# Row sums of softmax numerators: from full columns on 128 partitions to folded strips of 64 rows by 32 columns

## The chip, the cores and the metric

The kernel runs on one core of a Trainium2 chip. The metric is the time of one execution on the device in microseconds (us), of which three runs were made. Five engines work side by side, each on its own queue in order: PE (TensorE, with its weight loads as PEld), DVE (VectorE), ACT (ScalarE), POOL (GpSimd) and SP (SyncE, here only for issuing DMAs).

## What is computed

Four graph layers on 32 samples of 512 nodes with 256 features, all in fp32, each behind a layernorm and a relu and added to its input:

```python
h = max(layernorm(x), 0); x = x + attention(h, adj)            # layer 0: 4 heads of 64
h = max(layernorm(x), 0); x = x + two_gats_with_mlps(h, adj)   # layer 1
h = max(layernorm(x), 0); x = x + gat(h, adj, 4 heads of 64)   # layer 2, elu at the end
h = max(layernorm(x), 0); x = x + gat(h, prior=adj, 8 heads of 32) @ W_out.T   # layer 3
```

In each of them softmax numerators p (node j by node i, for each head) are multiplied with values, and the result is divided by the sums of p over j. The change is about those sums in layers 0, 2 and 3.

## The kernel before

A sample is worked on feature-major: tiles of 128 partitions by 512 nodes. For one head, p is four tiles p[j], with j on the partitions (four blocks of 128) and the 512 nodes i along the free dimension. The product with the values contracts over the partitions, four matmuls into one PSUM bank (`av`). The row sums contract in the same way with a matrix of ones: first the four p[j] are added elementwise to one tile, `total`, and then one matmul with 32 columns of ones gives the 512 sums on 32 partitions. Four heads take four column strips of the array, so four such matmuls fill one bank `sm` (a unit of four; in the profile eight passes, since an fp32 product takes two).

The names and lines to follow:
- `layer0` (L694): for m in 0, 1, two heads each: scores `sc` in two row strips of 64, exp on ACT, the mask and the additions to `total` on DVE, the products `av` in two column strips of 64. Then one `sm` unit for all four heads and `normalise`.
- `normalise` (L669): copies `sm` and `av` out of PSUM, sends the sums through DRAM to 128 partitions (`s1`, `few`), inverts them, sends them back (`s2`) and out to all partitions (`rc`), and multiplies.
- `separable` (L858), for layers 2 and 3: for each group g of four heads (one group in layer 2, two in layer 3) and each j, ACT makes exp tiles from the broadcast `R`, DVE takes the maximum with the second branch and masks. For g = 0 the additions to `total` are DVE's; for g = 1 they are accumulating DMAs that POOL issues, into p[0] (`p<-p` in the profile). The last sample of layer 2 and the last two of layer 3 take the sums directly from the p[j] with ones on TensorE (`direct`).
- `norm_t` (L609): layernorm; its power of -0.5 (`rs`) is a POOL instruction.

The order of the work is not the order of this code. Every operation is recorded as a step (`Plan`, L71) and `Plan.order` (L157) chooses, with costs from `cost` (L319), the step that can start first, ties by a due time; a sample's due time is its number times `PERIOD`, less the work behind the step and less a number from the table `URGENT`. Samples and layers are released at `STARTS`, `PACE` and `LAYERS`. At most `AHEAD` + 1 samples are in flight. A step that opens a new tile has to get a buffer: 62 common SBUF blocks of 128 by 512, eight PSUM banks, 4 tiles x of a sample's residual; some are held back for older samples (`KEEP`, `OWN`). All instructions are then issued in that order (`issue`, L267), so that nearly all carry line L283.

Of the kernel before, what the change touches and what calls it, by code (L numbers as in the profile page):

```python
# [43 lines left out]

PERIOD = 179.0
STARTS, PACE = (0.0, 0.0, 38.0, 159.0), 85.0
LAYERS = (0.0, 4.0, 2.0, 98.0)

URGENT = {
    "pt:0": 192, "mm:0": 49, "total:0": 70, "av:0": 68, "mm:1": 25, "total:1": -78, "rs1:1": 42, "av:1": -7,  # L50
    "p2:1": 104, "p3:2": -95, "total:2": -542, "ue:2": -396, "mv:3": -121, "mm:3": -158, "p3:3": -723,
    "av:3": -527, "total:3": -695,
}
BLOCKS, KEEP = 62, 2
KEEP_BANKS = 0
# [15 lines left out]
class Plan:  # L71
# [8 lines left out]
    ENGINES = dict(tensor="PE", vector="DVE", scalar="ACT", gpsimd="POOL", sync="SP")  # L80
    HOP, AHEAD = 0.05, 3

    OWN = dict(block=8, bank=2)

    SWITCH = dict(full=0.094, columns=0.12, rows=0.2)
# [71 lines left out]
    def order(self):  # L157
# [35 lines left out]
        def slots(step):  # L193

            when, taken = 0.0, {}
            for name in step.touches:
                if name in live:
                    continue
                tag = self.tile_tag[name]
                keep = self.tags[tag][1]  # L200
                reserve = 0
                for s in range(oldest, step.sample):
                    if to_come[s].get(tag, 0):
                        reserve += max(0, min(keep, to_come[s][tag] + held.get((s, tag), 0)) - held.get((s, tag), 0))
                n = taken.get(tag, 0)
                own = self.OWN.get(tag, 0)
                if own:
                    passed = bisect_left(pending[step.sample, tag], place[name]) - n
                    reserve += max(0, min(own, passed))
                if len(free[tag]) - n <= reserve:  # L210
                    return None
                when = max(when, sorted(free[tag])[n])
                taken[tag] = n + 1
            return when
# [104 lines left out]
def cost(engine, op, args, kw, out):  # L319
# [22 lines left out]
    if engine == "POOL":  # L342
        if op == "dma_start":
            return 1.1, (5.2 if n == N else 8.0)
        return (1.0 if n < 16 else 0.683), 0.1
# [7 lines left out]
def gnn_stack_kernel(ctx: ExitStack, tc: tile.TileContext, a: dict, out: bass.AP):  # L353
# [66 lines left out]
    def new_x():  # L420
        return first.tile([P, NT, D], F32, name="x", bufs=4)

# [160 lines left out]
    def pipelined(stack):  # L583
# [15 lines left out]
        def small(name, *free):  # L599
            return q.tile(big, [P, *free], name, 4)  # L600

        def half(b, t):

            return b[t // 2][:, t % 2 * D : (t % 2 + 1) * D]
# [64 lines left out]
        def normalise(avs, sm):  # L669


            raws, sums = blocks("raw", len(avs)), block("sums")
            q.scalar.copy(sums, sm)
            for raw, av in zip(raws, avs):
                q.scalar.copy(raw, av)
            s1, s2 = q.tile(dram, [4, N], "s1", 8), q.tile(dram, [4, N], "s2", 8)
            q.sync.dma_start(s1, sums[0:P:32, :])
            few = small("few", 2, 4 * NT)
            c = 4 * N // P
            q.sync.dma_start(few[:, 0, :], T(s1, "h (p c) -> (h p) c", c=c))  # L680
            q.vector.reciprocal(few[:, 1, :], few[:, 0, :])
            q.sync.dma_start(T(s2, "h (p c) -> (h p) c", c=c), few[:, 1, :])
            dst = blocks("oT", len(avs))
            per = 4 // len(avs)
            for i, raw in enumerate(raws):
                rc = block("rc")
                for h in range(per):
                    f = P // per
                    q.sync.dma_start(rc[h * f : (h + 1) * f, :], s2[i * per + h : i * per + h + 1, :].to_broadcast([f, N]))
                q.vector.tensor_tensor(dst[i], raw, rc, op=ALU.mult)  # L690
            return dst


        def layer0(xt):  # L694
            hT = norm_t(xt)
# [11 lines left out]
            rows = [slice(0, 64), slice(64, P)]  # L707
            avs, totals = [], []
            for m in range(KD):
                av = bank("av")  # L710
                avs.append(av)
                tot = blocks("total", 2)
                totals += tot
                p = {}
                for jj in range(0, NT, 2):
                    for j in (jj, jj + 1):
# [4 lines left out]
                        for s in range(2):  # L721
# [3 lines left out]
                            if j:  # L725
                                q.vector.tensor_tensor(tot[s], p[0, s] if j == 1 else tot[s], b, op=ALU.add)
                    with q.unit("columns", 1.72):
                        for j in (jj, jj + 1):
                            for s, r in enumerate(rows):
# [3 lines left out]
                                )  # L733
            sm = bank("sm")
            with q.unit("columns", 0.86):
                for n, b in enumerate(totals):
                    q.tensor.matmul(sm[n * 32 : n * 32 + 32, :], ones[:, :32], b, start=True, stop=True)
            oT = normalise(avs, sm)
            for t in range(0, NT, 2):
# [118 lines left out]
        def separable(xt, w, nh, mask, bars):  # L858
# [16 lines left out]
            q.sync.dma_start(T(rd[:nh, :], "h (t p) -> t h p", p=P), rT[: NT * nh, :])  # L875
            per = P // f
            for g in range(nh // 4):
                R = blocks("R", 4)
# [3 lines left out]
                direct = q.left <= (1 if nh == H2 else 2)  # L882
                total = blocks("total", 4) if g == 0 and not direct else None
                sm = bank("sm") if direct else None
                for j in range(NT):
                    p = blocks("p3", 4)
                    for s in range(4):
# [4 lines left out]
                        )  # L892
                        if j and total:
                            q.vector.tensor_tensor(total[s], first[s] if j == 1 else total[s], p[s], op=ALU.add)
                        elif j and not direct:
                            q.gpsimd.dma_start(out=first[s], in_=p[s], accum_op=ALU.add)
                    if not j:
                        first = p
                    st = dict(start=(j == 0), stop=(j == NT - 1))
                    with q.unit("columns", (0.86 if per == 4 else 1.72) + (0.86 if direct else 0)):  # L900
# [3 lines left out]
                        if direct:  # L904
                            for s in range(4):
                                q.tensor.matmul(sm[s * F3 : (s + 1) * F3, :], ones[:, :F3], p[s], **st)
                if not direct:
                    sm = bank("sm")
                    with q.unit("columns", 0.86):
                        for s, b in enumerate(total or first):  # L910
                            q.tensor.matmul(sm[s * F3 : (s + 1) * F3, :], ones[:, :F3], b, start=True, stop=True)
                bars(g, avs, sm)

        def layer2(xt):
            y = blocks("y3", 3)

            def bars(g, avs, sm):
                for b, ps in zip(y, avs + [sm]):
                    q.scalar.copy(b, ps)

            separable(xt, w2, H2, mask1T, bars)
# [17 lines left out]
        def layer3(xt):  # L939
            oT = []  # L940

            def bars(g, avs, sm):
                if q.left > 1:
                    oT.extend(normalise(avs, sm))
                    return
# [79 lines left out]
        for i in range(B):  # L1025
            q.begin()
            q.sample, q.left = i, B - i
            xt = q.adopt(new_x() if i else x0, "x", 4)
            if i:
# [434 lines left out]
```

## Time and profile before

| | |
|---|---|
| three runs | 3959.78, 3960.19, 3964.37 us; median 3960.19 |
| span of the profiled execution | 3962.9 us |
| mean granted TensorE clock | 0.992 |
| PE, DVE, ACT, POOL busy | 98%, 84%, 71%, 14% of the span |
| row sums after additions (`sm<-total`, `sm<-p`) | 1144 passes, 8 in a unit |
| POOL's accumulating DMAs `p<-p` | 360 |
| DMA traffic | 292.57 MB |

The profile is of one execution, whose span from first to last instruction stands in the second row, beside the times of the three runs. In its lines, an instruction is named by what it writes and reads (`sm<-total,ones`), with rows*columns of the array and the shapes; "x8" is a count; busy time is in us, the mean of one in ns. In the table of stretches each line has the stretch, its length, the busy time of PE, PEld, DVE, ACT and POOL with the number of instructions, the granted clock, the DMA share and GB/s. The timeline has start, length and what ran, with equal neighbours merged; two neighbours can overlap by the end of the pipeline, so that starts are compared with starts.

### The profile page before, as it was taken

How to read it: one execution, taken by the hardware profiler on the slowest of the kernel's cores; microseconds unless marked ns; L12 is line 12 of the kernel's file. 1: busy time of each engine (PE TensorE's matmuls, PEld its weight loads, DVE VectorE, ACT ScalarE, POOL GpSimd, SP SyncE). 2: the span in 40 equal slices, each digit the busy share in tenths (PEclk: the TensorE clock that was granted, in tenths of full speed). 3: DMA queues.
4: the chain of work that ended last, by engine and by line, in shares of the span. 5: the costliest groups of instructions: out<-in, count | busy, mean ns of one | idle time of the engine just before them, and what ended most of it. 6: DMA issues, size and time to landing. Idle time of an engine off the chain costs nothing.

```text
span 3962.9 us, 52558 instructions
## 1 busy us (share of the span) xinstructions
PE 3890.9 (98%) x17144; PEld 2149.1 (54%) x17144; DVE 3344.2 (84%) x7049; ACT 2805.9 (71%) x5968; POOL 566.4 (14%) x530
## 2 busy tenths in 40 slices
PE   8999999999999999999999999999999999999997
PEld 4655555555555555555555555555555555555552
DVE  6499898888888888988888988888888889888886
ACT  4577677766677766767766777666777667777665
POOL 0001111101111111111101111011111011111010
PEclk8999999999999999999999999999999999999998
DMA  3013333313233223333223333132332233332231
GB/s 101 21 37 81 72 82 84 92 44 92 57 89 92 71 65 76 76 84 84 67 63 78 76 88 88 49 89 59 86 92 73 63 76 76 84 83 69 71 77 50
DMA packets 217616, 292.57 MB, mean 74 GB/s; under 512 B 49915, under 2 KB 103422, under 8 KB 217334
## 3 DMA queue, kind: packets, MB, share of 16 engines
q0 software_dynamic: 68864, 111.18, 16.1%
q1 hardware_dynamic: 148196, 177.69, 14.3%
q8 instruction: 138, 2.26, 0.2%
q14 instruction: 144, 1.18, 0.1%
q10 hardware_dynamic: 274, 0.26, 0.0%
HBM read 158.79 MB, written 19.10 MB: 45 GB/s over the span
## 4 chain that ended last, share of the span: by engine, by line
PE 69%; DVE 17%; DMA 5%; ACT 4%; issue 2%; POOL 2%; SPq 1%; DVEq 0%; ACTq 0%; POOLq 0%
PE mm L283 33%; PE av L283 22%; PE sc L283 5%; PE pt L283 5%; DVE total L283 5%; DVE p L283 5%; DMA R<-rd 4%; PE sm L283 3%; ACT p L283 2%; POOL rs L283 2%; DVE o L283 1%; DVE ue L283 1%; DVE stats L283 1%; DVE x L283 1%; DVE y L283 1%
## 5 line engine op out<-in xcount | busy, mean ns | idle before, releaser
L283 ACT ACTIVATE p<-R,e 128x512 f32<-128x512 f32 x1536 | 993.4, 727 | 53.2 <-DMA R<-rd 52.3
L283 PE MATMUL av<-p,v 128*128 128x512 f32 (+1 forms) x2560 | 930.8, 596 | 4.5 <-DVE p L283 4.4
L283 DVE SCALAR_TENSOR_TENSOR p<-p,e,mask3T 128x512 f32<-128x512 f32 x1024 | 720.5, 749 | 8.1 <-ACT p L283 8.1
L283 POOL TENSOR_TENSOR rs<-ve,mhalf 128x4 f32<-128x4 f32 x128 | 202.5, 1582 | 2755.9 <-DVE ve L283 2634.4
L283 PEld LDWEIGHTS av<-p,v 128*128 128x128 f32 (+1 forms) x2560 | 348.2, 169 | 446.5 <-issue 357.2
L283 DVE TENSOR_TENSOR total<-total,p 128x512 f32<-128x512 f32 x872 | 572.6, 687 | 1.4
L283 PE MATMUL av<-p,vs 128*32 128x512 f32 (+1 forms) x3072 | 504.5, 598 | 5.6 <-DVE p L283 5.4
L283 PE MATMUL mm<-W_fc,o 128*128 128x256 f32 (+1 forms) x2048 | 468.4, 380 | 2.8 <-ACT o L283 2.8
L283 PEld LDWEIGHTS mm<-W_fc,o 128*128 128x128 f32 x2048 | 382.5, 190 | 85.3 <-issue 29.4
L283 POOL DMA_DIRECT2D p<-p x360 | 323.9, 1047 | 564.2 <-PE av L283 191.2
L283 DVE SCALAR_TENSOR_TENSOR p<-p,e,mask1T 128x512 f32<-128x512 f32 x512 | 350.7, 748 | 41.0 <-ACT p L283 40.4
L283 ACT ACTIVATE h<-x,ms,rs 128x256 f32<-128x256 f32 x512 | 280.1, 628 | 122.9 <-DVE ms L283 121.0
L283 DVE TENSOR_TENSOR p<-p,mask0T 128x512 f32<-128x512 f32 x512 | 328.5, 690 | 17.4 <-ACT p L283 17.2
L283 PEld LDWEIGHTS av<-p,vs 128*32 128x32 f32 (+1 forms) x3072 | 138.4, 118 | 342.2 <-issue 238.6
L283 DVE TENSOR_TENSOR total<-p,p 128x512 f32<-128x512 f32 x436 | 288.7, 687 | 0.0
L283 ACT ACTIVATE p<-sc 128x512 f32<-128x512 f32 x512 | 254.3, 679 | 7.8 <-PE sc L283 7.8
L283 PE MATMUL mm<-w,hT 128*128 128x272 f32 (+1 forms) x1024 | 254.4, 393 | 0.9 <-ACT hT L283 0.8
L283 PE MATMUL mm<-hT,mlp_w 128*128 128x512 f32 x512 | 237.6, 596 | 0.0
L283 PE MATMUL mm<-o,mlp_w 128*128 128x512 f32 x512 | 234.7, 596 | 1.3
L283 PE MATMUL sc<-qT,kT 64*128 64x512 f32 x1024 | 230.1, 599 | 0.0
L283 PEld LDWEIGHTS mm<-w,hT 128*128 128x128 f32 x1024 | 190.6, 191 | 61.0 <-issue 15.3
L283 ACT COPY rc<-pt 128x512 f32<-128x512 f32 x64 | 37.4, 585 | 246.8 <-PE pt L283 246.7
(183 smaller groups left out, 5457.5 us busy)
## 6 DMA issues: line engine op xcount, KB each, us to landing
R<-rd SPq DMA_DIRECT2D x384, 256.0 KB
p<-p POOLq DMA_DIRECT2D x360, 256.0 KB, 5.3
x<-in_x_dram SPq DMA_DIRECT2D x32, 512.0 KB
x<-boa POOLq DMA_DIRECT2D x32, 512.0 KB, 5.5
rc<-s SPq DMA_DIRECT2D x128, 128.0 KB
out_dram<-x SPq DMA_DIRECT2D x32, 512.0 KB
rc<-s SPq DMA_DIRECT2D x248, 64.0 KB
s<-sums SPq DMA_DIRECT2D x94, 8.0 KB
```

The lines of the kernel that those rows point to most:

```text
L283: getattr(getattr(self.nc, attribute), op)(*args, **kw)
```

## The change

Ahead of the row sums, the total is folded onto half of its partitions. In layers 0 and 2 the totals of two heads stand in one tile `pair` (128 partitions, two halves i of 256 nodes, two heads, 256). `fold` issues two accumulating DMAs from POOL: for i = 0 the upper 64 partitions are added to the lower 64, for i = 1 the lower to the upper. `folded` then takes eight matmuls of 64 rows, 32 columns and 256 nodes, two row strips by four column strips, into two banks. In layer 3, group g's totals are folded onto half g, and the row sums of both groups are taken together, in one unit of eight matmuls of 512 nodes; `normalise8` does the two groups in one.

Beside that, the planner's numbers change: 48 common blocks, 6 pairs (two blocks in size each) and 5 tiles x in place of 62 blocks and 4 tiles x; one more sample in flight; four blocks and two banks kept spare while an older sample still needs some; other release times and a longer table `URGENT`; and another cost of a POOL DMA. So all instructions get another order.

```diff
-PERIOD = 179.0
-STARTS, PACE = (0.0, 0.0, 38.0, 159.0), 85.0
-LAYERS = (0.0, 4.0, 2.0, 98.0)
+PERIOD = 193.0
+STARTS, PACE = (0.0, 0.0, 46.0, 123.0), 94.0
+LAYERS = (0.0, 8.0, 88.0, 61.0)
...
-BLOCKS, KEEP = 62, 2
+BLOCKS, KEEP = 48, 2
+PAIRS = 6
+LOW = slice(0, 64), slice(64, 128)
...
-    HOP, AHEAD = 0.05, 3
+    HOP, AHEAD = 0.05, 4
...
+    SPARE = dict(block=4, bank=2)
...
+                if any(to_come[s].get(tag, 0) for s in range(oldest, step.sample)):
+                    reserve += self.SPARE.get(tag, 0)
...
-            return 1.1, (5.2 if n == N else 8.0)
+            return 1.1, 3.9 + n * out.ap[0][1] * 4 / 190e3
...
-        return first.tile([P, NT, D], F32, name="x", bufs=4)
+        return first.tile([P, NT, D], F32, name="x", bufs=5)
...
+        def pair(name):
+            b = q.tile(big, [P, 2, 2, N // 2], name, PAIRS, keep=2, tag="pair")
+            return b, [b[:, :, s, :] for s in range(2)]
+        def wide(b):
+            return T(b, "p (i c) -> p i c", i=2)
+        def fold(b):
+            for i in range(2):
+                q.gpsimd.dma_start(out=b[LOW[i], i], in_=b[LOW[1 - i], i], accum_op=ALU.add)
+        def folded(pairs):
+            sm = [bank("sm"), bank("sm")]
+            with q.unit("columns", 0.44):
+                for n in range(4):
+                    for i, r in enumerate(LOW):
+                        q.tensor.matmul(
+                            sm[i][n * F3 : (n + 1) * F3, : N // 2], ones[r, :F3], pairs[n // 2][r, i, n % 2, :],
+                            start=True, stop=True,
+                        )
+            return sm
...
-            q.scalar.copy(sums, sm)
+            if isinstance(sm, list):
+                for i in range(2):
+                    q.scalar.copy(sums[:, i * D : (i + 1) * D], sm[i][:, :D])
...
+        def normalise8(raws, sms):
+            s1, s2 = q.tile(dram, [2, 4, N], "s1x", 3), q.tile(dram, [2, 4, N], "s2x", 3)
+            for g, sm in enumerate(sms):
+                sums = block("sums")
+                q.scalar.copy(sums, sm)
+                q.sync.dma_start(s1[g], sums[0:P:32, :])
+            few = small("fewx", 2, 8 * NT)
...
-            sm = bank("sm")
-            with q.unit("columns", 0.86):
-                for n, b in enumerate(totals):
-                    q.tensor.matmul(sm[n * 32 : n * 32 + 32, :], ones[:, :32], b, start=True, stop=True)
-            oT = normalise(avs, sm)
+                fold(both)
+            oT = normalise(avs, folded(totals))
...
-                            q.gpsimd.dma_start(out=first[s], in_=p[s], accum_op=ALU.add)
+                            q.gpsimd.dma_start(out=total[s], in_=p[s], accum_op=ALU.add)
...
+                    raw = block("raw")
+                    q.scalar.copy(raw, avs[0])
+                    for b in both:
+                        q.gpsimd.dma_start(out=b[LOW[g]], in_=b[LOW[1 - g]], accum_op=ALU.add)
+                    late.append((raw, total))
+            if late:
+                sms = [bank("sm"), bank("sm")]
+                with q.unit("columns", 0.86):
+                    for s in range(4):
+                        for g, r in enumerate(LOW):
+                            q.tensor.matmul(
+                                sms[g][s * F3 : (s + 1) * F3, :], ones[r, :F3], late[g][1][s][r, :],
+                                start=True, stop=True,
+                            )
+                bars(0, [raw for raw, _ in late], sms)
```

## The prediction

> **What bounds the kernel now.** I read the page's table of engines first, then the busy time by stretches, then TensorE's timeline in the middle of the run, then the groups of instructions.
>
> ```profile
> PE 3890.9 (98%) x17144; PEld 2149.1 (54%) x17144; DVE 3344.2 (84%) x7049; ACT 2805.9 (71%) x5968; POOL 566.4 (14%) x530
> ```
> ```profile
> 0.00:100.00 100.00, 84.56 (x333) 43.62 (x334) 59.52 (x152) 44.72 (x82) 9.62 (x16) 0.90 0.36 102
> ...
> 1000.00:1500.00 500.00, 498.24 (x2208) 273.61 (x2205) 435.36 (x905) 367.92 (x791) 79.76 (x76) 1.00 0.33 76
> ...
> 3800.00:3900.00 100.00, 86.18 (x430) 38.41 (x427) 81.98 (x187) 62.73 (x134) 3.04 (x3) 0.94 0.14 44
> 3900.00:3963.00 63.00, 41.24 (x187) 19.77 (x187) 33.67 (x47) 25.57 (x52) 0.00 (x0) 0.80 0.20 61
> ```
>
> Between 200 and 3800 us TensorE is busy 99.6% of the time at full clock, VectorE 87%, ScalarE 74%. So the middle is TensorE's; a microsecond of it removed is a microsecond gained until something else is late. Only the first 200 and the last 160 us are set by chains.
>
> ```profile
> 2000.17 0.27 PE L283 MATMUL pt<-ident,mx 128*128 128x128 f32 x1
> 2000.37 1.06 PE L283 MATMUL sm<-p,ones 128*32 128x512 f32 x8
> 2001.36 11.82 PE L283 MATMUL av<-p,vs 128*64 128x512 f32 x64
> 2013.00 2.02 PE L283 MATMUL sm<-total,ones 128*32 128x512 f32 x8
> 2014.95 1.53 PE L283 MATMUL pt<-ident,y 128*128 128x128 f32 x12
> ...
> 2027.29 7.03 PE L283 MATMUL av<-p,v 128*128 128x512 f32 x16
> 2034.16 0.59 PE L283 MATMUL mm<-woT,oT 128*128 128x256 f32 x2
> ...
> 2052.12 1.07 PE L283 MATMUL sm<-total,ones 128*32 128x512 f32 x8
> 2053.01 1.90 PE L283 MATMUL av<-p,vs 128*32 128x512 f32 x16
> ```
>
> Three prices come from these starts. Sixteen 512-column passes take 6.87 us, 0.429 each; a product is two passes, so four products side by side in four column strips have 0.853 us of streaming. The unit at 2052.12 is followed by one of the same array shape after 0.89: 0.037 us over, for the staggered starts. The unit at 2000.37 is followed by another shape after 0.99: a change of array shape costs about 0.095 us. At 2013.00 the unit takes 1.95, though it has the same work: it waits about 1 us for its totals.
>
> **Row sums: streaming removed.** The program has 32 row-sum units in layer 0, 31 in layer 2 and 60 in layer 3, 123 in all, besides 20 that the last samples take directly and that stay. Before: 123 x 0.853 = 105.0 us. After: layers 0 and 2 sum 256 columns in eight strips of 64 rows by 32 columns, 63 x 0.427 = 26.9; layer 3 has one unit of 512 columns in eight strips in place of two of four, 30 x 0.853 = 25.6. Saved: 52.5 us, if eight strips run at once. The trace shows two row strips at once (scores) and four column strips at once, not both.
>
> ```profile
> L283 PEld LDWEIGHTS sm<-p,ones x8: 106/108/109, 2000.4 to 2000.4; 128*32 128x32 f32 x8
> L283 PE MATMUL sm<-p,ones x8: 592/605/617, 2000.4 to 2000.8; 128*32 128x512 f32 x8
> ```
>
> These are that unit's weight loads and matmuls, with the first and last start: all eight loads begin within 0.1 us, and the second four matmuls by 0.43 us after the first. A new unit has sixteen of each. Against this stands a rule of the Trainium skill ("TensorE: Matmul & The Clock Gate", Part 1, "Wait — 56ns, not 53.3ns?"): matmuls never start less than about 25 ns apart, however small. By the rule eight starts would spread 0.2 us before each round of eight is on its way, and a unit would be about 0.2 us longer, 93 x 0.2 = 19 us of the saving. The row says otherwise: the 0.037 us over four strips is 9 ns a strip; with eight, 0.074. I take the row: 93 x 0.074 - 123 x 0.037 = +2.3 us.
>
> **Changes of shape: added.** Everything else on TensorE has the same matmuls; but the order is another. Laying the orders of the two programs' TensorE instructions side by side, the array changes shape 545 times before and 812 times after: the 64x32 strips are a shape of their own, and the layer-2 products, one stretch of 64 passes at 2001.36, stand one by one among full-array work. 267 x 0.095 = +25.4 us.
>
> **The sum.** Streaming of all matmuls is 3690.7 us before (2684.6 full array, 438.6 in 64-column, 347.4 in 32-column, 218.5 in 64-row strips, 1.8 the rest), changes of shape 545 x 0.095 = 51.8; the span 3962.9 leaves 220.4 for both ends, small starts and waits. After: 3638.3 + 77.1 + 2.3 + 220.4 = 3938.1, that is 24.8 less. The span is 2.7 above the median of the runs; applied to the median, 3935.4.
>
> **What the sum puts at nothing, and its cover.** POOL's work:
>
> ```profile
> L283 POOL DMA_DIRECT2D p<-p x360 | 323.9, 1047 | 564.2 <-PE av L283 191.2 <-ACT ew L283 142.0 <-DMA p<-p 96.5
> L283 POOL TENSOR_TENSOR rs<-ve,mhalf 128x4 f32<-128x4 f32 x128 | 202.5, 1582 | 2755.9 <-DVE ve L283 2634.4 <-DVE few L283 47.7 <-DVE sq L283 36.1
> p<-p POOLq DMA_DIRECT2D x360, 256.0 KB, 5.3
> ```
>
> The change adds 128 + 124 + 120 = 372 folding DMAs. At 1.047 us each that is 389 us on POOL, 14% becoming 24%. A fold waits for its total or for the accumulating DMA before it, and behind it on POOL are the `rs` powers of the layernorms, whose h and transposes wait. But in the new order the layer-3 folds stand just after their own accumulations, the others in a group before the same sample's `rs`, which needs them anyway; so no other sample's norm is held for long. A fold lands some 5 to 7 us after issue (the row's 5.3 for the same bytes; 4 KB on each of 64 partitions may take longer). In the order there are 70 us of matmul time between layer 0's last product and its row sums, 21 us in layer 2, 11 us in layer 3. In layer 3 two landings in series (accumulate, fold: 12 to 14 us) have to fit; they begin at the last `p`, ahead of the product, so I count zero; were 2 us missing each time, 30 x 2 = 60 us would go. Without any cover one fold is 6 us in each of 93 places.
>
> DMA traffic grows by 252 x 131 KB + 120 x 262 KB = 64 MB on 293 MB, and queues are busy 31% of the time. VectorE has the same additions, now on two pieces of 256; ScalarE takes four half copies for two full ones in layers 0 and 2, (4 x 0.41 - 2 x 0.586) / 2 = 0.23 us a unit, 15 us at 71% busy. The layer-3 normalisation sends fewer small DMAs through SP, two a sample less. All that is covered by TensorE's 99.6%; uncovered it is 15 us at most, and below nothing only where the row sums' own wait of 1 us (2013.00) disappears, as the row sums now stand 21 us after the last product: at most 31 x 1 = 31 us.
>
> The ends: the last samples keep the direct sums, and from the last sample's layer 2 on TensorE has 56 us of matmul time before and 60 after, in the same chain that takes 107 us (3855.5 to 3962.9). The start has the same loads and the first samples in nearly the same order, one fold more. Zero, 10 us either way.
>
> **Rivals.**
> (a) The sum, 3935. Its own range is 3922 to 3948.
> (b) The waits of the row sums go too and nothing takes their place: 3935 less most of the 31 us, 3910. For it: the distances above. Against: a wait ended leaves TensorE early at the next tight place.
> (c) New small waits eat what was won, within 8 us of before: 3958.
> (d) Slower: banks. Row sums hold two PSUM banks instead of one, five samples share eight. Counting matmul time between the last matmul of a bank's old content and the first of its new one, no reuse in the middle has under 2 us in the old order; in the new, eight per sample have, the shortest 1.5. Emptying takes 0.17 us of matmul end (592 ns recorded for 427 of streaming), 0.586 of copy, and 0.727 if one exponential stands ahead on ScalarE: 1.48. If these eight wait 0.2 us each beyond what they do now, 51 us: 3986. It decides from 24.8 / 32 = 0.78 us of new waits per sample. Against it: ScalarE is idle a quarter of the time, and a late TensorE lets it catch up.
> (e) The strips don't run eight at once, but in two rounds: the 52.5 us come back, 3988.
>
> **How the numbers follow.** (a) 0.48, (b) 0.20, (c) 0.10, (d) 0.17, (e) 0.05. I take 0.2%, 8 us, as what a measurement of this kernel can tell from no change. Faster: (a), (b) and part of (c), 0.70; same 0.10; slower 0.20. The range reaches from 3902 (somewhat under (b), if the ends gain) to 3986, the price of (d), with about half of (d) and (e) beyond it.
>
> **What would show it.** Right: row-sum units of 16 passes in layers 0 and 2 followed after 0.5 to 0.65 us, in layer 3 after 0.95 to 1.05; TensorE's passes up from 17144 to 17648 with its busy time down about 25; POOL near 950 us. Wrong: units of 0.85 us and more (e); TensorE idle or weight loads waiting on ScalarE's copies in the middle, under 98.5% busy (d); row sums waiting for a DMA (the folds' cover fails); a tail longer than 107 us after the last sample's layer 2.

## The result, and the profile after

The changed kernel takes 4030.56 us (median of four runs, 4029.22 to 4034.98), beside 3961.44 us for the kernel before on the same chip: a ratio of 1.0175 (95% interval 1.0161 to 1.0189), 69 us slower. The profiled execution has a span of 4027.3 us, where the sum had given 3938.1.

First the table of engines, as for the kernel before:

```profile
PE 3899.6 (97%) x17648; PEld 2121.8 (53%) x17648; DVE 3336.3 (83%) x7019; ACT 2832.3 (70%) x6031; POOL 863.9 (21%) x902
```

TensorE has the 17648 passes that were counted, but its busy time went up by 8.7 us instead of down by 25. Next the same stretches (length, busy time of PE, PEld, DVE, ACT, POOL, then granted clock, DMA share, GB/s):

```profile
0.00:100.00 100.00, 86.76 (x366) 47.52 (x368) 58.67 (x149) 45.59 (x84) 17.83 (x25) 1.00 0.43 111
1000.00:1500.00 500.00, 492.24 (x2233) 268.88 (x2233) 424.61 (x900) 359.85 (x778) 114.47 (x118) 1.00 0.43 93
3800.00:3900.00 100.00, 89.75 (x392) 48.15 (x391) 79.90 (x164) 70.47 (x153) 20.64 (x23) 0.95 0.38 80
3900.00:4028.00 128.00, 92.11 (x465) 42.71 (x463) 82.23 (x144) 72.40 (x152) 2.36 (x2) 0.83 0.21 64
```

The clock in the middle is full in both, and the start is no worse. In the middle TensorE was busy 498.24 of 500 us and is now busy 492.24. VectorE is busy 425 instead of 435 us and ScalarE 360 instead of 368; only POOL, which issues the folds, is busier (114 instead of 80 us). So no engine has become the busy one there; work comes later. One stretch near the end shows the rest, 3700 to 3800 us, first before, then after:

```profile
3700.00:3800.00 100.00, 99.51 (x451) 59.02 (x450) 85.17 (x189) 75.61 (x159) 15.97 (x15) 1.00 0.33 83
```
```profile
3700.00:3800.00 100.00, 91.00 (x423) 48.79 (x422) 87.16 (x189) 61.80 (x134) 23.76 (x27) 1.00 0.40 80
```

TensorE begins to stand idle some 100 us earlier than it did, although the run ends 64 us later.

The row sums themselves are in TensorE's timeline of the changed kernel (start, length, what ran):

```profile
2040.21 1.53 PE L299 MATMUL sm<-total,ones 64*32 64x512 f32 x16
2041.67 3.65 PE L299 MATMUL av<-p,vs 128*64 128x512 f32 x16
...
2063.70 0.66 PE L299 MATMUL sm<-total,ones 64*32 64x256 f32 x16
2064.30 1.13 PE L299 MATMUL mm<-L_WoT,oT 128*128 128x256 f32 x4
```

Start to start, a unit of eight strips of 256 columns takes 0.60 us (0.59 in the mean of all 63), within the 0.5 to 0.65 that was forecast: eight strips of 64 by 32 do run at once. Layer 3's unit takes 1.46 here (mean 1.38), where 0.95 to 1.05 was forecast: it waits some 0.4 us for the folds, for without them it takes 1.02 in every sample (run 3 below).

What TensorE waited for, in pauses above 0.15 us, summed from 260 to 3660 us (engine, what it waited to run, whose result; us in total, times, longest), before and after:

```profile
PE mm L283 <- ACT o L283: 8.0, 16, 1.9
PE mm L283 <- ACT hT L283: 3.8, 14, 0.3
PE av L283 <- DVE p L283: 2.8, 3, 1.3
```
```profile
PE av L299 <- DVE p L299: 29.7, 77, 0.9
PE pt L299 <- DVE nd L299: 21.9, 28, 0.9
...
PE sm L299 <- DMA total<-total: 0.2, 1, 0.2
```

14.6 us of named waits have become 52.6 (a line of 0.8 us, one pause, is left out). They stand at three places that come once in almost every sample: the transposes of the second GAT's exp factor ew2 (`ew` in the profile), behind VectorE's `nd`, and products that wait for numerators p in two layers. The name p does not tell the layer, but the shapes do; the groups of instructions in the same stretch (after the bar: busy us, mean ns, idle us before them) show layer 1's products first, then layer 3's:

```profile
L299 PE MATMUL av<-p,v 128*128 128x512 f32 x1344 | 625.9, 595 | 15.3 <-DVE p L299 15.1
L299 PE MATMUL av<-p,vs 128*32 128x512 f32 x1568 | 213.1, 596 | 14.6 <-DVE p L299 14.6
```

None of these is a wait for ScalarE to empty a bank, and the row sums are hardly in the list. One sample's layer-3 place in the timeline (in brackets the idle time ahead of the instruction, and its releaser):

```profile
2006.12 1.89 PE L299 MATMUL av<-p,vs 128*32 128x512 f32 x14
2008.35 1.07 PE L299 MATMUL av<-p,vs 128*32 128x512 f32 x8 [0.33 <-DVE p L299]
2009.61 1.04 PE L299 MATMUL av<-p,vs 128*32 128x512 f32 x2 [0.20 <-DVE p L299]
2010.59 1.09 PE L299 MATMUL pt<-ident,h 128*128 128x128 f32 x8
```

Layer 1's place comes later in the same stretch. The first line is from the chain that ended last (start, length, what), the others are from the timeline of all engines:

```profile
2024.91 11.53 DMA total<-p
```
```profile
2036.46 2.56 ACT L299 ACTIVATE p<-R,e 128x512 f32<-128x512 f32 x4 [1.46 <-DMA total<-p]
2037.22 1.42 DVE L299 SCALAR_TENSOR_TENSOR p<-p,e,mask1T 128x512 f32<-128x512 f32 x2 [1.88 <-ACT p L299]
...
2045.41 1.01 DVE L299 TENSOR_SCALAR p<-r,ew 128x512 f32<-128x512 f32 x2
...
2046.01 3.70 PE L299 MATMUL av<-p,v 128*128 128x512 f32 x8 [0.69 <-DVE p L299]
```

One accumulating DMA of layer 3 takes 11.53 us from issue to landing. Only then does ScalarE write a further p: none of its inputs comes from such a DMA, so it must be the block, which the DMA was still reading. This p is of layer 2 (it is masked by `mask1T`, layer 3's by `mask3T`). From there VectorE works through its queue without a pause above 0.15 us to the p of layer 1's first GAT (`p<-r,ew`), and TensorE's products wait 0.69 us for that. How long ScalarE stood idle for such landings between 260 and 3660 us, before and after:

```profile
ACT p L283 <- DMA p<-p: 0.6, 1, 0.6
```
```profile
ACT p L299 <- DMA total<-p: 40.9, 52, 2.3
ACT qT L299 <- DMA total<-p: 28.0, 28, 1.8
ACT v L299 <- DMA total<-p: 10.0, 26, 1.1
```

Before, the longest of these 360 DMAs took 9.4 us from issue to landing and nine in ten were in within 8.1; after, 12.4 and 10.5. The chain's shares have turned over as well: PE 69% and DVE 17% before, DVE 47% and PE 27% after.

### The profile page after: what moved, and what is told of

Its sections match the earlier page's. It is cut to its first block, busy times and chain, and to the rows that moved or that the text cites. A ratio compares the mean times of both kernels' runs of the same rounds, so it can differ in the third digit from the quotient of the medians.

```text
span 4027.3 us, 54834 instructions
## 1 busy us (share of the span) xinstructions
PE 3899.6 (97%) x17648; PEld 2121.8 (53%) x17648; DVE 3336.3 (83%) x7019; ACT 2832.3 (70%) x6031; POOL 863.9 (21%) x902
## 4 chain that ended last, share of the span: by engine, by line
DVE 47%; PE 27%; ACT 9%; DMA 7%; issue 5%; POOL 5%; DVEq 0%; SPq 0%; POOLq 0%; ACTq 0%
DVE p L299 18%; PE mm L299 15%; DVE total L299 15%; PE av L299 7%; DMA total<-p 7%; DVE stats L299 4%; POOL rs L299 3%; DVE x L299 3%; ACT h L299 3%; ACT e L299 2%; PE pt L299 2%; ACT p L299 2%; DVE ue L299 2%; POOL total L299 1%; DVE y L299 1%
## 5 line engine op out<-in xcount | busy, mean ns | idle before, releaser
L299 ACT ACTIVATE p<-R,e 128x512 f32<-128x512 f32 x1416 | 931.1, 725 | 90.7 <-DMA total<-p 44.1
L299 PE MATMUL av<-p,v 128*128 128x512 f32 (+1 forms) x2560 | 960.6, 599 | 23.1 <-DVE p L299 22.7
L299 DVE SCALAR_TENSOR_TENSOR p<-p,e,mask3T 128x512 f32<-128x512 f32 x904 | 631.3, 748 | 82.0 <-ACT p L299 80.7
L299 PEld LDWEIGHTS av<-p,v 128*128 128x128 f32 (+1 forms) x2560 | 339.0, 169 | 410.0 <-issue 330.9
L299 POOL TENSOR_TENSOR rs<-ve,mhalf 128x4 f32<-128x4 f32 x128 | 193.8, 1514 | 1597.5 <-DVE ve L299 1190.9
L299 POOL DMA_DIRECT2D total<-total x372 | 315.9, 970 | 992.2 <-DVE total L299 470.3
L299 DVE SCALAR_TENSOR_TENSOR p<-p,e,mask1T 128x512 f32<-128x512 f32 x512 | 360.0, 750 | 131.2 <-ACT p L299 125.2
L299 POOL DMA_DIRECT2D total<-p x360 | 327.8, 1134 | 494.2 <-PE av L299 235.1
L299 PEld LDWEIGHTS av<-p,vs 128*32 128x32 f32 (+1 forms) x2832 | 129.5, 119 | 366.4 <-issue 208.0
L299 PE MATMUL mm<-o,mlp_w 128*128 128x512 f32 x512 | 226.3, 593 | 2.1 <-DVE o L299 2.1
```

The costliest lines, as they stand in the source:

```text
L299: getattr(getattr(self.nc, attribute), op)(*args, **kw)
```

## The experiments

Ratios are to the kernel before, run beside each on the same chip. "Places" A and B are two of the three waits above: A the ew2 transposes, B layer 3's products. The third, layer 1's products, got no run of its own.

**1 and 2: row sums and order apart.** One kernel has the new row sums with the old planning numbers, the other the old row sums with the new numbers, each with as many blocks as fit:

```diff
 # 1, against the changed kernel (and the old PERIOD, STARTS, LAYERS, URGENT, 4 tiles x)
-BLOCKS, KEEP = 48, 2
+BLOCKS, KEEP = 50, 2
-    HOP, AHEAD = 0.05, 4
+    HOP, AHEAD = 0.05, 3
-    SPARE = dict(block=4, bank=2)
+    SPARE = dict()
 # 2, against the kernel before (and the new PERIOD, STARTS, LAYERS, URGENT, SPARE, 5 tiles x)
-BLOCKS, KEEP = 62, 2
+BLOCKS, KEEP = 60, 2
-    HOP, AHEAD = 0.05, 3
+    HOP, AHEAD = 0.05, 4
```

> The new row sums (pairs, folds, strips of 64 by 32) with the old planning numbers: old release times and URGENT, four samples in flight, 4 tiles x, no spare buffers; 50 common blocks, so that SBUF is as before. Theory A (the folding and accumulating DMAs land late and hold up ACT, DVE and POOL): slower than before here too, 3990 to 4030. Theory B (the new order of the work loses by itself, whatever the row sums are): the row sums' saving is seen, 3900 to 3945.

> The old row sums with the new planning numbers: new release times and URGENT, five samples in flight, 5 tiles x, spare buffers; 60 common blocks. Theory A: no folds, so about as before, 3950 to 3985. Theory B: as slow as the changed kernel or slower by the row sums' 50 us, 4020 to 4090.

They took 4531.34 us (1.1445, 1.1425 to 1.1464) and 4152.2 us (1.0485, 1.0467 to 1.0502). Both expectations were far off. As I read it, the planning numbers fit one set of steps each, and with another set the order is bad (TensorE is busy 453.62 of 500 us in the first); so these two do not split the change. From here on the changed kernel's own order was kept, and single instructions were taken out of it.

**3 to 7: the folds, and what they lean on.** In the loop that issues the steps (in 5 and 6, ScalarE's copies into `sums` and `y3` also add a one):

```diff
+    # 3: no folds (the row sums then add half of the nodes j only); 4: the same for layer 3 alone
+    if attribute == "gpsimd" and op == "dma_start" and kw["in_"].tensor.name == kw["out"].tensor.name:
+        continue
+    # 5: as 3, and layer 3's accumulating DMAs left out as well
+    if step.layer == 3 and attribute == "gpsimd" and op == "dma_start":
+        continue
+    # 6: as 3, and the additions to total of layers 0, 2 and 3 on VectorE left out as well
+    if step.layer != 1 and attribute == "vector" and op == "tensor_tensor" and self.kinds.get(args[0].tensor.name) == "total" and args[0].tensor.name == args[1].tensor.name:
+        continue
+    # 7: layer 3's folds over 16 of 1024 columns (the others stay unfolded)
+    kw = dict(kw, out=kw["out"][:, :16], in_=kw["in_"][:, :16])
```

> The changed kernel with all instructions in their places, but its 372 folding DMAs left out (the row sums then miss half of the rows). Theory A: most of the loss goes, 3935 to 3970. Theory B: the order is the same, so 4015 to 4030.

> The changed kernel with only the 120 folds of layer 3 left out (256 KB each on 64 partitions; layer 3's row sums then miss half of the rows). Theory A, as the late landings are seen in layer 3: nearly as fast as without any fold, 3940 to 3980. If the many small folds of layers 0 and 2 count: 3990 to 4015. Theory B: 4015 to 4030.

> The changed kernel's order with neither the 372 folds nor layer 3's 360 accumulating DMAs (its sums miss rows; the copies of the sums add one so that no inverse is infinite). If what is left of the loss without folds (3997) is still DMAs that land late and hold the blocks of p: 3940 to 3970. If it is the order of the other engines' work: 3985 to 4000.

> The changed kernel's order without the folds and without 744 of VectorE's additions to the totals of layers 0, 2 and 3 (the sums miss rows; the copies of the sums add one). If TensorE's waits that stay without the folds are waits for VectorE, which does its queue in order: 3930 to 3960, the sum of the prediction. If they are for other things (DMAs, banks, ScalarE): 3980 to 4000.

> The changed kernel with the 120 folds of layer 3 in their places and with their waits, but only 16 of the 1024 columns wide, 4 KB instead of 256 KB (layer 3's row sums then miss half of the rows for the most part). If the folds cost by their traffic, or by the time their bytes take: as without them, 3990 to 4005. If they cost by the waits and the fixed time of one more DMA in series: 4015 to 4030.

| | us | ratio (interval) | less than the change |
|---|---|---|---|
| 3, no folds | 3996.93 | 1.0088 (1.0071 to 1.0105) | 34 |
| 4, no folds in layer 3 | 3994.68 | 1.0084 (1.0067 to 1.0101) | 36 |
| 5, no folds, no accumulations | 3985.85 | 1.0058 (1.0041 to 1.0075) | 45 |
| 6, no folds, no additions | 3985.14 | 1.0052 (1.0035 to 1.0069) | 45 |
| 7, thin folds in layer 3 | 3997.28 | 1.0084 (1.0067 to 1.0101) | 33 |

Run 3 lies between its two expectations: the folds cost 34 us, about half of the loss. All of it is layer 3's: run 4, which keeps the 252 folds of layers 0 and 2, is as fast as run 3 (its time lies where the small folds were expected to count, but leaving them out as well wins nothing more). Runs 5, 6 and 7 came out as one of their expectations has it, the second, the second and the first. Run 7 still issues every fold and its row sums still depend on them, but with 4 KB each in place of 256, and the 34 us are gone all the same. So it is the time that the folds' bytes take.

Where TensorE gains it is seen in the same groups without folds, layer 1's products, then layer 3's, then layer 3's row sums, and last those row sums with folds:

```profile
L301 PE MATMUL av<-p,v 128*128 128x512 f32 x1360 | 633.8, 595 | 1.1 <-DVE p L301 1.1
L301 PE MATMUL av<-p,vs 128*32 128x512 f32 x1568 | 212.9, 596 | 14.7 <-DVE p L301 14.7
L301 PE MATMUL sm<-total,ones 64*32 64x512 f32 x448 | 30.5, 601 | 0.0
```
```profile
L299 PE MATMUL sm<-total,ones 64*32 64x512 f32 x448 | 40.8, 600 | 0.5 <-DMA total<-total 0.2
```

Layer 3's products wait as long without folds as with them (14.7 and 14.6 us): place B is not the folds' doing. What goes is the wait of layer 1's products and that of the row sums. Counted from start to start in the same stretch, beyond streaming and changes of shape, layer 1's products lose 29 us with folds and 14 without, the row sums 11 less, and layer 3's output products, which need the row sums, 19 and 11: 34 in all. So the folds cost in two ways. Layer 3's row sums wait for the folds themselves, and the accumulating DMAs on the same queue land later: nine in ten within 10.5 us and the longest in 12.4, but within 9.0 and 11.0 without folds. With later landings layer 2's p, and behind them layer 1's, get their blocks later; ScalarE's idle time for landings, 78.9 us above, is 32.4 without folds.

Run 5, without the accumulations too, and run 6, which takes 511 us of additions off VectorE (73% busy), win 11 to 12 us more and no longer show ScalarE waiting for an accumulating DMA. A and B stay even so: in run 6 21.9 us at A, as in the changed kernel, and 14.3 at B, where it has 14.6. VectorE's load is not what TensorE waits for there.

**8 to 10: the two waits taken away.** In 8 and 9 the instruction reads a constant in place of the late operand:

```diff
+    # 8: place A (leaves that factor out of the second GAT)
+    if attribute == "tensor" and op == "transpose" and self.kinds.get(args[1].tensor.name) == "ew2":
+        args = (args[0], self.one, args[2])
+    # 9: place B (leaves layer 3's products out)
+    if attribute == "tensor" and step.layer == 3 and self.kinds.get(args[0].tensor.name) == "av":
+        args = (args[0], args[1], self.filler)
+    # 10: both, and no folds as in 3
```

> The changed kernel in its own order, but in layer 1 the transposes of the second GAT's exp factor read a constant of ones in place of it (that factor of the second GAT is left out); the same TensorE instructions, with nothing to wait for at this place, where 0.94 us a sample go. Theory (the new order puts instructions on TensorE's queue too close behind the VectorE results that they read, and the two places add up): 4031 - 30 x 0.94 = 4003 us. Rival (another engine or the buffers pace the loop, and a wait removed here turns up at the next place): 4026 to 4033 us.

> The changed kernel in its own order, but layer 3's products read a constant tile in place of the numerators p (the products are left out of layer 3; the row sums still read their totals). TensorE has the same passes and waits for no p at this place, where 1.28 + 0.53 us a sample go. Theory (waits put there by the order, which add up): 4031 - 30 x 1.81 = 3977 us. Rival (the wait turns up at the next place, since something else paces the loop): 4026 to 4033 us.

> The changed kernel in its own order with the folds left out and both waits taken away as in the two kernels before (the row sums add only half of the nodes j, layer 3's products and a factor of the second GAT are left out). Theory (all three are independent terms: folds 34, the ew2 transposes 28, the layer-3 products 54): 4031 - 116 = 3915 us, and the predicted 3938 lies above it since about 0.8 us a sample of such waits was in the old order too. Rival (something else paces the loop at 3985 to 3997, where the kernels without folds came to lie): 3985 us or above.

They took 4032.14 (1.0179, 1.0162 to 1.0196), 3983.9 (1.0058, 1.0041 to 1.0075) and 3979.78 us (1.0042, 1.0025 to 1.0059). The theory that the places add up fell with the first. At A nothing is won, although its wait is gone from the list:

```profile
PE av L301 <- DVE p L301: 30.0, 78, 1.1
PE pt L301 <- ACT h L301: 5.4, 30, 0.3
PE sm L301 <- DVE total L301: 4.7, 26, 0.2
```

The waits for p are what they were, and small waits stand where A's was. B gives 47 of the 54 us expected. But A, B and the folds together give 51, where 47 and 34 would be 81: the gains overlap. In run 10 layer 1's products wait 20.2 us although there are no folds (18.3 in run 9), and VectorE waits for landings ahead of the p of their first GAT, first run 9, then run 10:

```profile
DVE p L301 <- DMA total<-p: 50.5, 27, 2.9
```
```profile
DVE p L305 <- DMA total<-p: 51.0, 27, 2.6
```

With B gone TensorE comes to layer 1's products earlier, and these then wait for blocks that the accumulating DMAs hold, with or without folds. That this sets the 3980 us of run 10 is my reading; another limit near 3980 is not ruled out. Why the new order puts layer 3's products so close behind their p was not tried either. Place A is slack: TensorE waits elsewhere if not there.

**11: the order mended by hand.** Everything is computed. At three places a sample TensorE's matmuls that could already run are put ahead of the one that waits: at A three layer-0 output products, ahead of the fourth unit at B four products of layer 1, and one unit of layer-1 products ahead of another that waits for p. `w` is the waiting step, `m` a later one of TensorE whose inputs are planned to be ready 1 us ahead of it.

```diff
-        steps, at = self.order(), {}
+        steps, at = self.filled(self.order()), {}
+    FILL = {(1, "pt", "ew2"): (0, 1.0), (3, "av", "vs"): (3, 1.7), (1, "av", "v1"): (4, 0.8)}
...
+                if not all(b in moved or where[id(b)] < at and (b.engine == "PE" or b.start + b.lasts + 1.0 < w.start) for b in m.before):
+                    continue
...
+            for m in moved:
+                steps.remove(m)
+            i = steps.index(w)
+            steps[i:i] = moved
```

> The whole changed kernel with everything computed, and only TensorE's order mended at three places a sample: three layer-0 output products ahead of the ew2 transposes, four products of layer 1 ahead of the fourth unit of layer-3 products, one unit of layer-1 products of another head ahead of the unit that waits for p. Theory (instructions wait because of where the order put them, while others that could run stand behind them): of 0.94 + 1.28 + 0.78 us a sample most goes, less two changes of array shape, 0.19: 4031 - 30 x (3.0 - 0.19) = 3947 us at best, and 3960 to 3990 if about half of it comes back elsewhere. Rival (the waits are at the pace of VectorE and only move): 4020 to 4040 us.

4085.77 us (1.0314, 1.0297 to 1.0331), 55 us worse. The waits of A and B went down, but others, which had not been there, came:

```profile
PE pt L342 <- ACT h L342: 25.8, 27, 1.0
PE pt L342 <- ACT es L342: 21.5, 27, 1.8
PE mm L342 <- DVE oT L342: 10.9, 44, 0.4
...
PE av L342 <- DVE p L342: 8.8, 27, 0.3
```

This missed both expectations. My reading is that work put ahead of an instruction for which other engines wait makes these later, even where it fills a wait of TensorE's; which of the three moves did it was not tried.

**12 and 13: TensorE free of operands, in both orders.** Every matmul and transpose of samples 4 to 31 reads one constant (nothing is computed there); shapes, banks and all other engines' work stay. In these samples TensorE then waits for banks only.

```diff
+    if attribute == "tensor" and 4 <= step.sample < 32:
+        flat = []
+        for ap in args[1:]:
+            n = 1
+            for _, c in ap.ap[1:]:
+                n *= c
+            p0, p1 = extent(ap)[:2]
+            flat.append(self.filler[p0 : p1 + 1, :].to_broadcast([p1 - p0 + 1, n]))
+        args = (args[0], *flat) if op == "matmul" else (args[0], flat[0], args[2])
```

> The changed kernel in its own order, with every matmul and transpose of samples 4 to 31 reading a constant in place of its operands (so those samples compute nothing of the layers); shapes, banks and all other engines' work as they were. TensorE then waits only for its banks. To be read against the same kernel of before. Theory (the prediction's terms for streaming and shapes hold, and the loss is TensorE waiting for operands in a ring through VectorE and the accumulating DMAs): 25 us below the kernel of before treated in the same way, about 3870 to 3900 us. Rival (TensorE's own stream or the emptying of banks is what got longer): above the kernel of before treated in the same way, 3960 us or more.

> The kernel before in its own order, with every matmul and transpose of samples 4 to 31 reading a constant in place of its operands (so those samples compute nothing of the layers). TensorE then waits only for its banks. Streaming 3690.7, shapes 51.8, the start 41.6 and about 2.5 us a sample of small starts that are no waits: 3860 to 3920 us, whichever theory holds; it is the measure for the changed kernel treated in the same way.

The changed kernel takes 3920.71 us so (0.9893, 0.9877 to 0.9910), which misses the 3870 to 3900 expected; the kernel before takes 3911.95 (0.9876, 0.9860 to 0.9893). TensorE is hardly ever idle in the middle of either; changed kernel first, then before:

```profile
1000.00:2000.00 1000.00, 999.06 (x4599) 551.90 (x4598) 872.16 (x1826) 747.92 (x1608) 242.06 (x250) 1.00 0.46 97
```
```profile
1000.00:2000.00 1000.00, 1000.00 (x4484) 557.33 (x4481) 882.40 (x1834) 733.18 (x1579) 158.11 (x149) 1.00 0.34 78
```

So the emptying of banks hardly holds TensorE up there. Late operands cost 110 us in the changed kernel and 50 in the one before: 60 of the 69 us. But the remaining difference is +9 us where my terms for TensorE's own stream say -25. Between 1000 and 3600 us the starts of these two traces give, beside the streaming at 0.427 us for 512 columns, 82 us for 362 changes of array shape before and 118 us for 572 after, all small starts included: 210 more changes go with 36 more us, 0.17 each, not 0.095.

The pair also separates TensorE's waits from its stream. I counted, in all four traces, the time from the first start to the last between 260 and 3660 us, beyond streaming and beyond 0.095 a change (such counts are good to a few us). Before: 106.6 us, of which 69.7 stay with TensorE free; the rest, 36.9, are waits for operands. After: 175.1, of which 94.5 stay; waits 80.6.

**14: a shorter TensorE in the old order.** The kernel before, with the row sums of samples 4 to 29 in layers 0, 2 and 3 taken over half of the columns; ScalarE's copy reads that half twice (so half of the sums are left out), and the order stays.

```diff
+    if attribute == "tensor" and op == "matmul" and 4 <= step.sample < 30 and step.mode == "columns" and self.kinds.get(args[0].tensor.name) == "sm":
+        if not any(self.kinds[name] == "av" for name in step.touches):
+            args = (args[0][:, : N // 2], args[1], args[2][:, : N // 2])
+    if op == "copy" and 4 <= step.sample < 30 and step.layer != 1 and self.kinds.get(args[1].tensor.name) == "sm":
+        args = (args[0].rearrange("p (i c) -> p i c", i=2), args[1][:, None, : N // 2].to_broadcast([P, 2, N // 2]))
```

> The kernel before in its own order, with the row sums of samples 4 to 29 in layers 0, 2 and 3 taken over 256 of the 512 columns and copied twice (half of the sums are left out): 104 units x 0.427 = 44 us less streaming on TensorE, nothing else changed. Theory (before the change TensorE was the pace by a wide margin, and only the new order has another ring beside it): 3961 - 44 = 3917 us. Rival (rings through VectorE and the accumulating DMAs lie close under TensorE's time in the old order too, so that a shorter TensorE gains little whatever the order): 3940 to 3961 us.

3939.85 us (0.9942, 0.9926 to 0.9959): 22 of the 44 us. Here too the middle shows where the other half went, first the kernel before, then this one:

```profile
1000.00:2000.00 1000.00, 994.22 (x4391) 551.62 (x4388) 865.50 (x1800) 730.01 (x1561) 158.65 (x148) 1.00 0.33 77
```
```profile
1000.00:2000.00 1000.00, 990.85 (x4439) 553.96 (x4439) 873.58 (x1817) 732.91 (x1569) 157.23 (x148) 1.00 0.34 78
```

TensorE is idle 9 us in 1000, where it was 6. Counted from start to start as above, 18 us have been added between 260 and 3660 us, spread over many places. The result lies at the near edge of the rival's expectation: TensorE, 99.6% busy between 1000 and 1500 us, led by a narrow margin, and half of what is taken from it comes back as waits, in the old order and without a single fold. An order planned anew for shorter row sums might keep more; that was not tried.

**15: the price of a change of shape.** Run 13 again, with 149 full-array matmuls of 256 columns each taken as two side by side in strips of 64 columns: same streaming, same banks, 294 more changes of shape.

```diff
+    if attribute == "tensor" and 4 <= step.sample < 32 and step.layer == 1 and "o1" in {self.kinds[name] for name in step.touches}:
+        self.full += 1
+        if self.full % 6 == 3 and args[0].ap[0][1] == P and args[1].ap[-1][1] == P:
+            for r in (slice(0, 64), slice(64, P)):
+                self.nc.tensor.matmul(args[0][r], args[1][:, r], args[2], **kw)
+            continue
```

> The kernel before with TensorE free of operands, as it was run just now at 3911.95 us, but 149 full-array matmuls of 256 columns in layer 1 are each taken as two side by side, in two strips of 64 columns: the same streaming and banks, 294 more changes of array shape (545 become 839). By the prediction's price, 0.095 us a change: 3940 us. By the price that the two kernels free of operands show together (in 2600 us of the middle 210 more changes go with 36 us more beside the streaming, 0.17; over all changes 0.21 to 0.23): 3912 + 294 x 0.17 to 0.21 = 3962 to 3974 us.

3959.56 us (0.9993, 0.9983 to 1.0002), 47.6 above run 13, which ran on another chip (46 by the ratios): 0.16 us a change, in which the 149 further matmuls are included. For these changes the prediction's price is ruled out.

## Why the prediction was wrong, point by point

- **Streaming removed, 52.5 us: right.** The units take 0.59 us in layers 0 and 2, and layer 3's take 1.02 where no fold holds them up; eight strips stand side by side, so (e) is out. The row's small stagger was a better guide than the prediction's rule of 25 ns: the eight starts at 2063.70 us come 7 ns apart. (The 1144 passes in the table of the time before are the 123 units and the 20 direct ones.)
- **Changes of shape, +25.4: mechanism and count right, price too low.** Taken alone, a change costs 0.162 us (run 15), so 267 of them cost 43. The 0.095 came from one pair of starts, from 32-column to 64-column strips; with TensorE free of operands a change from the full array to 32-column strips takes 0.37 us on average in the old order (70 of them), all small starts of the stretch before it included. So by this price TensorE's own stream is 7 us shorter (52.5 - 43.3 - 2.3), not 25.
- **"The span 3962.9 leaves 220.4 for both ends, small starts and waits", held constant: this step failed.** It became 309.6 (4027.3 less 3638.3, 77.1 and 2.3). Of the 89.2 us more, 43.7 are waits for operands in the middle (80.6 - 36.9), 20.7 are the ends (to 260 us 2.7 less, from 3660 us on 23.4 more), 17.9 are the shapes' price (267 x 0.067), and 6.9 are not placed.
- **"I count zero" for the folds: this failed too, for layer 3.** They cost 34 us in the whole run, and some 30 of the 44 us of waits in the middle go with them. A fold of layer 3 did land 6.1 us after its issue in the median, as counted, but one in ten took more than 10, and in the sample shown 15.6 us passed from the last accumulation's issue to the landing of its fold, where 12 to 14 were counted. So the cover fails by 0.36 us a sample (1.38 against 1.02 a unit), 11 us, and layer 3's output products come 8 us later. The 15 us at layer 1's products were not foreseen at all: the accumulating DMAs hold blocks that other layers wait for, and the folds delay them. For layers 0 and 2 zero was right.
- **Rival (d), slower: right side (3986 against 4031), wrong mechanism, so right by luck.** Tight reuse of banks costs nothing that runs 12 and 13 could show; the waits are for p and ew2. Its threshold, 0.78 us of new waits a sample, was a useful one: new waits came to 44 us over some 27 samples, 1.6 each.
- **Rival (b), the 1 us waits of the old row sums vanish: in layers 0 and 2 they did**, and what it was warned against came true: new waits took their place.
- **The tail.** From the last sample's layer 2 to the end it is 109 us, near the 107 given. The 23 us more stand ahead of it, between 3700 and 3900 us, where the samples in flight run out together. With TensorE free of operands 15 of them remain (from 3660 us on 69.5 us beyond stream and shapes against 54.7). Why was not tried.
- **What would show it.** TensorE under 98.5% busy in the middle was named as the mark of (d); 492.24 of 500 is 98.4%. Row sums waiting for a DMA was named as well, and they do. The marks were right, but the causes have to be read from the lists of waits. POOL came to 864 us, not 950, with no weight in the outcome; and between 200 and 3800 us TensorE and ScalarE were busy 99.5 and 73% before the change, not 99.6 and 74.

In sum: the prediction took all that it did not count as unchanged, while the order of all instructions was new. TensorE's own stream came out 9 us longer instead of 25 shorter, by the price of a change of shape and by the end; 60 us are operands that come later. Of these, the folds' bytes take 34, and B's place in the order 47 by itself, but the two overlap. Open are the end's 23 us, why the new order has B and A, and what sets the 3980 us that remain without them. No version that computes everything beat the kernel before.

## What to carry to other kernels

An engine that is 99.6% busy may lead the others by very little: before a microsecond taken off it is counted as won, one such microsecond should be taken off alone (here half came back). A term "all the rest, unchanged" is a prediction too when the whole order changes. Bytes put on a queue delay all that lands through it: ask which buffers those landings free, and who takes them next, as it can be another layer. Before a wait is given to a cause, find out which layer's instruction it is, and whether it goes when the cause goes: B did not go with the folds, although it too waits for a p. A price for something that happens 267 times should come from many places or from a run that adds it alone, not from one pair of starts.

## What the runs showed of the hardware

- Eight matmuls in strips of 64 rows by 32 columns run side by side: 256 columns in fp32 take 0.59 us start to start for all eight, and the eight starts come 7 ns apart (changed kernel, 2063.70 us).
- A change of array shape costs 0.16 us where full-array work is broken by two 64-column strips (run 15: 294 changes and 149 more matmuls, 47.6 us); one start after a change, from 32-column to 64-column strips, showed 0.095.
- Accumulating DMAs of 256 KB land 3.2 to 12.4 us after issue (median 5.2). With the 252 folds of 128 KB and 120 of 256 KB on the same queue the slowest tenth begins at 10.5 us, with 4 KB in place of the 256 at 9.2, without the 120 at 8.1, without any folds at 9.0.
- A TensorE that reads one constant in samples 4 to 31, with all other engines' work kept, still needs 3912 us of 3962: 50 us is what late operands cost there before the change; after it, 110.
